# Unread products in TensorE's gaps, and batch-norm statistics eight tiles behind, in the last two graph layers

## The chip, the cores and the metric

The kernel runs on one core of a Trainium2 chip. The metric is the device time of one execution in microseconds (us); lower is better. Engines are named as in the profile: PE (TensorE), DVE (VectorE), ACT (ScalarE), POOL (GpSimd), SP (SyncE). PSUM is the memory that PE writes its products to[...]; SBUF holds everything else.

## The reference

A network of four layers on a graph of 3125 nodes with 256 features and 50,000 edges, all in f32. Each layer is a graph step and a feed-forward step. The change touches the graph steps of layers 2 and 3:

```python
def _L2_gnn_ref(h, w, snorm_n, edge_src, edge_dst, W_self, W_func, W_att):
    h_s = h @ W_self.T
    z = h @ W_func.T
    e = leaky_relu(concatenate([z[edge_src], z[edge_dst], w]) @ W_att.T)[:, 0]
    m = segment_max(e, edge_dst, num_segments=N)
    e_exp = exp(e - m[edge_dst])
    alpha = e_exp / segment_sum(e_exp, edge_dst)[edge_dst]
    agg = segment_sum(alpha[:, None] * z[edge_src], edge_dst)
    h_new = relu(where(deg > 0, h_s + agg, h))
    return h + h_new

def _L3_gnn_ref(x, edge_index, W_proj, b_proj, W_l, b_l, W_r, gamma, beta):
    xp = relu(x @ W_proj.T + b_proj)
    agg = segment_max(xp[src], dst)              # over the edges into a node, itself included
    out = relu(agg @ W_l.T + b_l + x @ W_r.T)
    # then a batch norm: mean and variance of each feature over all nodes, gamma, beta
```

Around them, `x = x + gnn(layernorm(x))`. Layer 2's feed-forward step is a mixture of 16 experts, two per node; layer 3's has 8.

## The kernel before, in words

**Tiles and rounds.** The nodes are sorted by in-degree and cut into 25 tiles of 128 (one node per partition). Edges are handled in *rounds*: round r of a tile takes the r-th in-edge of each of its 128 nodes. A tile has `RND[t]` rounds, from 32 for the first tile to 9 for the last, 413 in all; `OFF[t]` is a tile's first round. One round is one indirect DMA issued by POOL (`gather`, L138): 128 rows of a table in HBM land in one SBUF row buffer. Edges beyond a tile's rounds are handled apart.

**Order.** The order of instructions on each engine is the order in which the program records them. In layer 2 a small planner (`class Plan`) settles it while the kernel is built. Each chain of work is a generator that yields its next step as an engine, a planned duration and what it needs; the planner keeps a free time for each engine, takes the step that can start first (on a tie of 0.05 us the chain of lower rank), records it, and adds a delay to its end (0.35 us for PE). Buffers that several chains use are `Ring`s, whose slots hold the planned time at which they come free. The chains are:

- `gathers()`: the 413 gathers of layer 2 into blocks of 4 rows (`g_rows`), for all tiles in the order `order2`.
- `attend()`: for each tile transposes the normalised features (`tp`, copied by ACT to `a_xt`), multiplies them with `W_self` on PE (`pu`, L2250, in a PSUM bank of its own), forms the edge scores on DVE, their exponential on ACT (`g_e`, L2271), the sum of weights and the division on DVE, adds the self-product (L2278, DVE reading `pu` in PSUM) and then adds each gathered row times its weight (L2283).
- `route2()`: layer norm, gate logits and the sorting of nodes to experts, for groups of tiles; `moved` is the time at which all of it is planned.
- `ex2.tokens()`, `ex2.weights(...)` and `experts2()`: the experts' loads, products and combination, in three chunks of tiles.

`pl.run(moved, ...)` runs them all up to the end of the routing; what is left of the experts runs in a second call, beside the projection that writes layer 3's table `tab3`.

**Layer 3** is a loop written out by hand over the 25 tiles. 24 gathers (`ROWS`) are issued ahead; then, for each round, DVE takes the running maximum (L2408) and POOL issues the gather 24 rounds further on (`look`), which needs that row buffer back. Before a tile's rounds PE transposes its features (`turned`, L1660, copied by ACT in L1662 to `g_xt`), after them the maxima (`g_at`); eight products (L2418 and L2420) and two ACT instructions (`c_y`, L2421) give the tile's outputs `Y`, features on the partitions. DVE's `bn_stats` of a finished tile (`stats`, L2397, two instructions of some 0.29 us) stands after the seventh round of a later tile, three tiles later (`LATE`); the last three tiles' statistics follow the loop, and then come the batch norm and the feed-forward step. PSUM there has three banks of `tp` and four of `mm`.

Of the kernel before, what the change touches and what calls it, by code (L numbers as in the profile page):

```python
# [9 lines left out]
F32 = mybir.dt.float32  # L10
# [25 lines left out]
ROWS = 24  # L36
W_BUFS = 2
GT = 5
LATE = 3
SLACK = 3.0  # L40
MM_COL = 0.0019
KEEP = max(1, N // 2) - 1
# [55 lines left out]
def tile_gnn_ffn(ctx: ExitStack, tc: tile.TileContext, a: dict, out: bass.AP):  # L98
# [7 lines left out]
    @contextmanager  # L106
    def psums(**bufs):
        with tc.tile_pool(name="psum", bufs=1, space=PSUM) as p:
            before = dict(banks)
            banks["pool"], banks["bufs"] = p, bufs  # L110
            yield
            banks.update(before)

    def ps(tag, shape):
        return banks["pool"].tile(shape, F32, name=tag, tag=tag, bufs=banks["bufs"][tag])
# [1586 lines left out]
    class Plan:  # L1702
# [4 lines left out]

        def __init__(self):
            self.free = {"PE": 0.0, "DVE": 0.0, "ACT": 0.0, "POOL": 0.0, "SP": 0.0, None: 0.0}
            self.wire, self.on, self.chains, self.born = 0.0, None, [], 0  # L1710

        def add(self, rank, chain):
            c = [rank, self.born, chain, None]
# [13 lines left out]
        def run(self, until=None, rings=()):  # L1727

            while self.chains:
                best, end = [], until is not None and until.t is not None  # L1730
                if end and not any(at.t is None for r in rings for at in r.slots):
                    break
                for c in self.chains:
                    engines, us, needs = c[3]
                    if end and any(isinstance(n, Ring) for n in needs):
                        continue
                    needs = [n if isinstance(n, float) else n.t for n in needs]
                    if None in needs:
                        continue
                    for k, engine in enumerate(engines if isinstance(engines, tuple) else (engines,)):  # L1740
                        best.append((max([self.free[engine], *needs]), k, engine, c))
                if not best:
                    raise RuntimeError([str(c[2]) + str(c[3]) for c in self.chains])
                first = min(b[0] for b in best)
                start, _, engine, c = min((b for b in best if b[0] <= first + 0.05), key=lambda b: (b[3][0], b[3][1], b[0], b[1]))
                self.free[engine], self.on = start + c[3][1], engine
                self.resume(c, start + c[3][1] + self.DELAY[engine])

# [409 lines left out]
    tab3 = dram.tile([NP, D], F32, name="tab3")  # L2158

    with tc.tile_pool(name="g2", bufs=2) as gp, \  # L2160
            tc.tile_pool(name="w2", bufs=1) as wp, psums(tp=2, mm=2, y=1, u=2, pu=1):
        ws = load_w(wp, a["L2_gnn_W_self"], "w_s")
        rw2 = load_w(wp, a["L2_ffn_gate_w"], "w_g")
        gb2 = bcast(a["L2_ffn_gate_b"], 16, wp, "w_gb")
# [49 lines left out]
                                                   op0=OP.mult, op1=OP.add)  # L2214
        rounds_beyond(wp, body2)

        order2 = list(range(NT - 1, CH2[2][1] - 1, -1)) + list(range(CH2[2][1]))
        pl = plan[0] = Plan()
        R = {"tp": Ring(2), "mm": Ring(2), "y": Ring(1), "u": Ring(2), "pu": Ring(1)}
        blocks = Ring(GR_BUFS)  # L2220
        xin, rows = {t: At() for t in order2}, {t: [] for t in order2}
        here, done, moved = {t: At() for t in order2}, {t: At() for t in order2}, At()
# [16 lines left out]
        def attend():  # L2239

            for t in order2:
                n = RND[t]
                xn = XN[:, t, :]
                xt = gp.tile([P, 2, P], F32, name="a_xt")
                f = yield from turned_steps(R["tp"], xt, xn, xin[t], 0.36)
                own = yield "PE", 2 * D * MM_COL, (f, R["pu"])
                pfree = R["pu"].take()
                pu = ps("pu", [P, D])
                for k in range(2):
                    nc.tensor.matmul(pu, xt[:, k, :], ws[:, k, :], start=(k == 0), stop=(k == 1))  # L2250
                h = gp.tile([P, D], F32, name="g_u")
                hf = yield "ACT", 0.5, (xin[t],)
                nc.scalar.activation(h, xn, AF.Copy, scale=hasnt[:, t : t + 1])
                e = gp.tile([P, RND[0] + 1], F32, name="g_e")
                nm = gp.tile([P, 1], F32, name="g_nm")
                dn = gp.tile([P, 1], F32, name="g_dn")
                u = ACC[:, t, :]
                while here[t].t is None:
                    yield None, 0.0, (here[t],)
                f = yield "DVE", 0.07, (here[t],)  # L2260
                nc.vector.tensor_copy(e[:, n : n + 1], M[:, t : t + 1])
                for r0, m, g, free, landed in rows[t]:
                    f = yield "DVE", 0.14, (landed,)
                    stt(e[:, r0 : r0 + m], g[:, :m, D], q2[:, t : t + 1], ewF[:, OFF[t] + r0 : OFF[t] + r0 + m],
                        op0=OP.add, op1=OP.add)
                f = yield "DVE", 0.51, (f,)
                stt(e[:, :n], e[:, :n], 0.01, e[:, :n], op0=OP.mult, op1=OP.max)
                nc.vector.tensor_reduce(nm, e[:, : n + 1], axis=AX.X, op=OP.max)
                nc.vector.tensor_scalar_mul(nm, nm, -1.0)
                f = yield "ACT", 0.3, (f,)  # L2270
                nc.scalar.activation(e[:, : n + 1], e[:, : n + 1], AF.Exp, bias=nm)  # L2271
                f = yield "DVE", 0.71, (f,)
                nc.vector.tensor_reduce(dn, e[:, :n], axis=AX.X, op=OP.add)
                stt(dn, den[:, t : t + 1], e[:, n : n + 1], dn, op0=OP.mult, op1=OP.add)
                nc.vector.reciprocal(dn, dn)
                nc.vector.tensor_scalar(e[:, : n + 1], e[:, : n + 1], dn, None, op0=OP.mult)
                f = yield "DVE", 0.41, (f, own)
                stt(u, u, e[:, n : n + 1], pu, op0=OP.mult, op1=OP.add)  # L2278
                pfree.t = f
                for r0, m, g, free, landed in rows[t]:  # L2280
                    f = yield "DVE", 0.52 * m, (f,)
                    for r in range(m):
                        stt(u, g[:, r, :D], e[:, r0 + r : r0 + r + 1], u, op0=OP.mult, op1=OP.add)  # L2283
                    free.t = f
                f = yield "DVE", 1.31, (f, hf)
                stt(u, u, has[:, t : t + 1], h, op0=OP.mult, op1=OP.add)
                stt(u, u, 0.0, xn, op0=OP.max, op1=OP.add)
                nc.vector.tensor_add(X[:, t, :], X[:, t, :], u)
                done[t].t = f
# [51 lines left out]
        with tc.manual_schedule(engines={EN.PE, EN.DVE, EN.Activation, EN.Pool, EN.SP}):  # L2341
            pl.add(2, gathers())
            pl.add(0, attend())
            pl.add(1, route2())
            pl.add(0, ex2.tokens())
            pl.add(0, ex2.weights((blocks, lambda: gp.tile([P, GB, ZW], F32, name="g_rows", bufs=GR_BUFS)
                                   .rearrange("p r d -> p (r d)"), here[order2[-1]])))
            ex2.out = "ACT"
            last = pl.add(4, experts2())
            pl.run(moved, R.values())  # L2350
            ex2.out = "ACT", "DVE"
            ex2.rest(range(NT))
            pl.meet(6.0)
            last[0] = 0
            order3 = ((20, 25), (15, 20), (10, 15), (6, 10), (3, 6), (0, 3))
            pl.add(3, ex2.fetch([t for g in order3 for t in range(*g)]))
            befores = [At(0.0), At(0.0)]
            for i, q in enumerate(order3):
                befores.append(At())
                pl.add(3 + i, table3(range(*q), f"t{i % 2}_", befores[i], befores[i + 2]))  # L2360
            pl.run()


    with tc.tile_pool(name="w3", bufs=1) as wp:
# [6 lines left out]
            return t  # L2371

        ga, be, bl = halves("c_ga", "L3_gnn_gamma"), halves("c_be", "L3_gnn_beta"), halves("c_bl", "L3_gnn_b_l")
        with tc.tile_pool(name="g3", bufs=2) as gp, psums(tp=3, mm=4):
            wl = load_w(gp, a["L3_gnn_W_l"], "c_wl")
            wr = load_w(gp, a["L3_gnn_W_r"], "c_wr")

# [18 lines left out]
                for i in range(2):  # L2396
                    nc.vector.bn_stats(bs[:, i, t, :], Y[:, i, t * P : t * P + h])  # L2397

            rows = {}
            with tc.manual_schedule(engines={EN.PE, EN.DVE, EN.Activation, EN.Pool, EN.SP}):  # L2400
                for r in range(ROWS):
                    look(r)
                for t in range(NT):
# [1 line left out]
                    xt = gp.tile([P, 2, P], F32, name="g_xt")  # L2405
                    turned(xt, XN[:, t, :])
                    for r in range(OFF[t], OFF[t + 1]):
                        nc.vector.tensor_tensor(u, u, rows.pop(r), op=OP.max)  # L2408
                        look(r + ROWS)
                        if t >= LATE and r == OFF[t] + 6:  # L2410
                            stats(t - LATE)
                    at = gp.tile([P, 2, P], F32, name="g_at")
                    turned(at, u)
                    for i in range(2):
# [4 lines left out]
                        for k in range(2):  # L2419
                            nc.tensor.matmul(py, wl[:, k, o], at[:, k, :], start=False, stop=(k == 1))  # L2420
                        nc.scalar.activation(Y[:, i, t * P : (t + 1) * P], py, AF.Relu, bias=bl[:, i : i + 1])  # L2421
                for t in range(NT - LATE, NT):
                    stats(t)


# [129 lines left out]
```

## Time and profile before

| | us |
|---|---|
| Median of 3 runs | 4231.69 (4225.03 to 4236.29) |
| The profiled execution, own time | 4194.93 |
| Its span, first to last instruction | 4193.1 |
| PE, DVE, POOL, ACT busy | 2681.7, 1935.3, 1758.2, 854.3 |
| Layer 2, gathers alone (2058 to 2380 us) | 322 |
| Layer 2, experts in three chunks and layer 3's table (2380 to 3149) | 769 |
| Layer 3, the gathering loop (3149 to 3747) | 598 |
| The rest of layer 3 (3747 to 4193) | 446 |

The profile is of one execution; stages are named by their place in its span. Busy is the time in which an engine worked. A group's line reads: kernel line, engine, operation, output<-inputs, shapes and count; then busy us in all, mean ns of one, and idle us just before them with what ended most of it. "remote" and "issue" are releasers that the profile can't place better: an event from elsewhere, or nothing that it shows. An f32 product of 128x256 appears as two rows. The mean granted TensorE clock over the span is 0.777 of full speed.

### The profile page before, as it was taken

The numbers are of one execution on the slowest core, as the hardware profiler recorded it, in microseconds if no ns is written. First come the engines' busy times: TensorE is split into PE (matmuls) and PEld (weight loads), VectorE is DVE, ScalarE is ACT, GpSimd is POOL, SyncE is SP. The second block draws the span as 40 slices with busy tenths as digits, with TensorE's granted clock in tenths as the row PEclk, the third lists the DMA queues.
The fourth block names the chain that finished last, engine by engine and source line by source line (L and its number), as shares of the span: only waits on it lengthen the run. The fifth ranks groups of instructions, "written<-read, shape, count | busy, mean of one in ns | idle before, by whom it ended". The sixth has DMA issues, their size and how long they took to land.

```text
span 4193.1 us, 46658 instructions
## 1 busy us (share of the span) xinstructions
PE 2681.7 (64%) x12940; PEld 2120.1 (51%) x12940; DVE 1935.3 (46%) x7465; ACT 854.3 (20%) x1839; POOL 1758.2 (42%) x1996
## 2 busy tenths in 40 slices
PE   1698999999889999948411366366670111137875
PEld 1576787777777878737310254254540011135653
DVE  4446666665665555442344433334563233245300
ACT  1121223221222233211100022022320000013321
POOL 4333334342253333002466545544337756633323
PEclk9678999989899999978755577577775555557987
DMA  6766455452243444113233355355523323323543
GB/s 220 230 185 205 129 149 159 124 149 63 81 125 102 118 131 128 52 48 107 74 95 93 84 177 177 90 173 173 177 83 104 103 76 91 94 74 109 161 159 101
DMA packets 275970, 521.46 MB, mean 124 GB/s; under 512 B 53608, under 2 KB 176896, under 8 KB 275684
## 3 DMA queue, kind: packets, MB, share of 16 engines
q0 software_dynamic: 105344, 306.57, 25.2%
q1 hardware_dynamic: 159466, 201.07, 15.5%
q10 hardware_dynamic: 10874, 10.54, 0.8%
q8 instruction: 114, 1.87, 0.2%
q14 instruction: 172, 1.41, 0.1%
HBM read 431.19 MB, written 86.78 MB: 124 GB/s over the span
## 4 chain that ended last, share of the span: by engine, by line
another core or an unknown queue 14%; PE 14%; issue 9%; DVE 6%; POOL 3%; DMA 3%; ACT 2%; DVEq 0%; POOLq 0%; ACTq 0%
PE y L1996 5%; PE mm L1992 5%; DVE ACC L2283 2%; DMA xg<-XX,ro_pos 1%; POOL xg L142 1%; PE tp L2047 1%; POOL g_row L138 1%; POOL ro_g L138 1%; PE u L1839 1%; DMA tab<-ACC,idI 1%; PE u L1984 1%; PE mm L2418 0%; ACT ro_h L2073 0%; PE tp L1777 0%
## 5 line engine op out<-in xcount | busy, mean ns | idle before, releaser
L138 POOL DMA_INDIRECT g<-tab,m_si x521 | 498.9, 958 | 978.7 <-DVE mt L897 527.7
L138 POOL DMA_INDIRECT g_rows<-tab,srcI x413 | 402.2, 974 | 287.5 <-DVE ACC L2283 124.6
L138 POOL DMA_INDIRECT g_row<-tab,srcI x413 | 397.7, 963 | 189.3 <-issue 111.1
L887 PEld LDWEIGHTS c<-s,g 128*128 128x128 f32 x2084 | 347.9, 218 | 150.1 <-issue 59.6
L887 PE MATMUL c<-s,g 128*128 128x96 f32 x2084 | 358.2, 301 | 84.1 <-issue 25.5
L894 PE MATMUL pw<-w_d,f 65*128 65x256 f32 x1042 | 375.6, 446 | 13.8 <-DVE mt L897 12.1
L926 PE MATMUL f<-w_rel,aT 128*126 128x256 f32 x1600 | 372.6, 383 | 0.0
L891 ACT COPY aT<-c 128x384 f32<-128x384 f32 (+1 forms) x323 | 236.7, 737 | 596.3 <-PE c L887 395.2
L926 PEld LDWEIGHTS f<-w_rel,aT 128*126 128x126 f32 x1600 | 300.0, 189 | 49.9 <-issue 5.4
L1992 PE MATMUL mm<-ro_xt,ro_w 128*128 128x192 f32 (+3 forms) x928 | 248.7, 420 | 101.9 <-ACT ro_h L2073 61.6
L897 DVE TENSOR_TENSOR mt<-pw,g 128x256 f32<-128x256 f32 x521 | 218.1, 419 | 164.6 <-PE pw L894 85.4
L1996 PE MATMUL y<-ro_w,ro_h 128*96 128x256 f32 (+2 forms) x1040 | 264.9, 410 | 39.9 <-issue 31.5
L2418 PE MATMUL mm<-g_xt,c_wr 128*128 128x128 f32 x200 | 48.6, 387 | 370.0 <-issue 259.3
L1992 PEld LDWEIGHTS mm<-ro_xt,ro_w 128*128 128x128 f32 x928 | 181.4, 218 | 152.1 <-ACT ro_h L2073 66.9
L2408 DVE TENSOR_TENSOR ACC<-ACC,g_row 128x256 f32<-128x256 f32 x413 | 174.0, 424 | 175.4 <-DMA g_row<-tab,srcI 145.2
L1996 PEld LDWEIGHTS y<-ro_w,ro_h 128*96 128x96 f32 (+2 forms) x1040 | 191.5, 190 | 93.2 <-issue 38.3
L2418 PEld LDWEIGHTS mm<-g_xt,c_wr 128*128 128x128 f32 x200 | 40.3, 281 | 377.8 <-issue 262.4
L1044 PE MATMUL w<-w,b_h 128*126 128x256 f32 x800 | 220.6, 401 | 7.3 <-issue 3.7
L142 POOL DMA_INDIRECT xg<-XX,ro_pos x100 | 101.8, 1018 | 292.4 <-issue 135.0
L2283 DVE SCALAR_TENSOR_TENSOR ACC<-g_rows,g_e,ACC 128x256 f32<-128x256 f32 x413 | 200.9, 486 | 47.8 <-DVE ACC L2283 21.6
L1035 PE MATMUL w<-xt,w 128*128 128x252 f32 (+1 forms) x832 | 218.7, 388 | 6.2 <-ACT xt L957 3.2
L894 PEld LDWEIGHTS pw<-w_d,f 65*128 65x128 f32 x1042 | 180.8, 217 | 17.0 <-DVE mt L897 14.2
(578 smaller groups left out, 4558.4 us busy)
## 6 DMA issues: line engine op xcount, KB each, us to landing
ro_w<-in_L_ffn_blocks SPq DMA_DIRECT2D x58, 514.0 KB
ro_w<-in_L_ffn_blocks SPq DMA_DIRECT2D x58, 512.0 KB
f<-in_attr_t SPq DMA_DIRECT2D x521, 32.5 KB
xg<-zero SPq DMA_DIRECT2D x78, 200.0 KB
b_at<-in_edge_attr SPq DMA_DIRECT2D x100, 125.0 KB
tabr<-v SPq DMA_DIRECT2D x12, 758.0 KB
g<-tab,m_si POOLq DMA_INDIRECT x521
g_rows<-in_L_ffn_blocks SPq DMA_DIRECT2D x14, 514.0 KB
```

Of the source, the lines that this page charges most:

```text
L138: return nc.gpsimd.indirect_dma_start(out=dst, out_offset=None, in_=table, in_offset=bass.IndirectOffsetOnAxis(ap=idx, axis=0))
L887: nc.tensor.matmul(pc[:, h, o : o + GW], g[:, h * P : (h + 1) * P], sums[k][0], start=True, stop=True)
L891: nc.scalar.copy(aT[:, :, :, b : b + n * GN].rearrange("p k r n -> p k n r"), pc[:, :, : n * GW].rearrange("p k (n r) -> p k n r", r=16))
L894: nc.tensor.matmul(pw, feats.pop(k), wd, start=True, stop=True)
L897: nc.vector.tensor_tensor(mt[0], pw, rows.pop(k)[:, D:], op=OP.mult)
L926: nc.tensor.matmul(cur["f"][:TN], aT[:, h, r, :], wrel[:, h, r, :], start=(r == 0 and h == 0), stop=(r == 15 and h == 1))
L1035: nc.tensor.matmul(ph, w["01"][:, e, k, i * P : (i + 1) * P], xt[:, k, : n * TN], start=(k == 0), stop=(k == 1))
L1044: nc.tensor.matmul(py, last[:, k, i * TN : (i + 1) * TN], w["02"][:, e - 1, k, :], start=(k == 0), stop=(k == 1))
L1992: nc.tensor.matmul(ph, w[:, o : o + P], xt[:, k, :], start=(k == 0), stop=(k == 1))
L1996: nc.tensor.matmul(py, h[:, i, s], w[:, i * D : (i + 1) * D], start=(i == 0), stop=(i == self.fc - 1))
L2283: stt(u, g[:, r, :D], e[:, r0 + r : r0 + r + 1], u, op0=OP.mult, op1=OP.add)
L2408: nc.vector.tensor_tensor(u, u, rows.pop(r), op=OP.max)
```

## The change

Layer 2 and layer 3 get products that nothing reads ("fills"), and layer 3's statistics move.

- *Layer 2.* Ahead of each step that it records on PE, the planner issues unread products of the identity with `W_self`, 512 columns each, into a PSUM bank `idle`: as many as 60% (`FILL`) of the gap since PE's previous step holds, at 0.9 us each. It does so up to the end of `pl.run(moved, ...)` only. The bank comes from `pu`: the self-product now goes to a slot of the ring `u`, ACT copies it to SBUF (`a_pu`, one buffer), and DVE reads it there.
- *Layer 3.* Ahead of each round's maximum PE multiplies the identity with the gathered row, 256 columns, twice, into one PSUM bank `idle`.
- *Layer 3's statistics.* `LATE` is 8. From tile 20 on a second tile's statistics stand after a tile's eleventh round where it has one (tiles 20, 21 and 22), so that 20 tiles' are in the loop and five follow it.

In the built order there are 184 fills in layer 2 and 826 in layer 3.

```diff
--- before.py
+++ after.py
@@ -36,7 +36,8 @@
 ROWS = 24
 W_BUFS = 2
 GT = 5
-LATE = 3
+LATE = 8
+FILL = 0.6
 SLACK = 3.0
 MM_COL = 0.0019
 KEEP = max(1, N // 2) - 1
@@ -1707,7 +1708,7 @@
 
         def __init__(self):
             self.free = {"PE": 0.0, "DVE": 0.0, "ACT": 0.0, "POOL": 0.0, "SP": 0.0, None: 0.0}
-            self.wire, self.on, self.chains, self.born = 0.0, None, [], 0
+            self.wire, self.on, self.chains, self.born, self.rest = 0.0, None, [], 0, None
 
         def add(self, rank, chain):
             c = [rank, self.born, chain, None]
@@ -1743,6 +1744,9 @@
                     raise RuntimeError([str(c[2]) + str(c[3]) for c in self.chains])
                 first = min(b[0] for b in best)
                 start, _, engine, c = min((b for b in best if b[0] <= first + 0.05), key=lambda b: (b[3][0], b[3][1], b[0], b[1]))
+                if engine == "PE" and self.rest is not None:
+                    for _ in range(int((start - self.free["PE"]) * FILL / 0.9)):
+                        self.rest()
                 self.free[engine], self.on = start + c[3][1], engine
                 self.resume(c, start + c[3][1] + self.DELAY[engine])
 
@@ -2158,7 +2162,7 @@
     tab3 = dram.tile([NP, D], F32, name="tab3")
 
     with tc.tile_pool(name="g2", bufs=2) as gp, \
-            tc.tile_pool(name="w2", bufs=1) as wp, psums(tp=2, mm=2, y=1, u=2, pu=1):
+            tc.tile_pool(name="w2", bufs=1) as wp, psums(tp=2, mm=2, y=1, u=2, idle=1):
         ws = load_w(wp, a["L2_gnn_W_self"], "w_s")
         rw2 = load_w(wp, a["L2_ffn_gate_w"], "w_g")
         gb2 = bcast(a["L2_ffn_gate_b"], 16, wp, "w_gb")
@@ -2214,9 +2218,12 @@
                                                    op0=OP.mult, op1=OP.add)
         rounds_beyond(wp, body2)
 
+        def rest():
+            nc.tensor.matmul(ps("idle", [P, 512]), ident, ws.rearrange("p k n -> p (k n)"), start=True, stop=True)
+
         order2 = list(range(NT - 1, CH2[2][1] - 1, -1)) + list(range(CH2[2][1]))
         pl = plan[0] = Plan()
-        R = {"tp": Ring(2), "mm": Ring(2), "y": Ring(1), "u": Ring(2), "pu": Ring(1)}
+        R = {"tp": Ring(2), "mm": Ring(2), "y": Ring(1), "u": Ring(2)}
         blocks = Ring(GR_BUFS)
         xin, rows = {t: At() for t in order2}, {t: [] for t in order2}
         here, done, moved = {t: At() for t in order2}, {t: At() for t in order2}, At()
@@ -2243,11 +2250,14 @@
                 xn = XN[:, t, :]
                 xt = gp.tile([P, 2, P], F32, name="a_xt")
                 f = yield from turned_steps(R["tp"], xt, xn, xin[t], 0.36)
-                own = yield "PE", 2 * D * MM_COL, (f, R["pu"])
-                pfree = R["pu"].take()
-                pu = ps("pu", [P, D])
+                f = yield "PE", 2 * D * MM_COL, (f, R["u"])
+                free = R["u"].take()
+                pw = ps("u", [P, 2, D])[:, 0, :]
                 for k in range(2):
-                    nc.tensor.matmul(pu, xt[:, k, :], ws[:, k, :], start=(k == 0), stop=(k == 1))
+                    nc.tensor.matmul(pw, xt[:, k, :], ws[:, k, :], start=(k == 0), stop=(k == 1))
+                own = free.t = yield "ACT", 0.42, (f,)
+                pu = gp.tile([P, D], F32, name="a_pu", bufs=1)
+                nc.scalar.copy(pu, pw)
                 h = gp.tile([P, D], F32, name="g_u")
                 hf = yield "ACT", 0.5, (xin[t],)
                 nc.scalar.activation(h, xn, AF.Copy, scale=hasnt[:, t : t + 1])
@@ -2276,7 +2286,6 @@
                 nc.vector.tensor_scalar(e[:, : n + 1], e[:, : n + 1], dn, None, op0=OP.mult)
                 f = yield "DVE", 0.41, (f, own)
                 stt(u, u, e[:, n : n + 1], pu, op0=OP.mult, op1=OP.add)
-                pfree.t = f
                 for r0, m, g, free, landed in rows[t]:
                     f = yield "DVE", 0.52 * m, (f,)
                     for r in range(m):
@@ -2345,10 +2354,10 @@
             pl.add(0, ex2.tokens())
             pl.add(0, ex2.weights((blocks, lambda: gp.tile([P, GB, ZW], F32, name="g_rows", bufs=GR_BUFS)
                                    .rearrange("p r d -> p (r d)"), here[order2[-1]])))
-            ex2.out = "ACT"
+            ex2.out, pl.rest = "ACT", rest
             last = pl.add(4, experts2())
             pl.run(moved, R.values())
-            ex2.out = "ACT", "DVE"
+            ex2.out, pl.rest = ("ACT", "DVE"), None
             ex2.rest(range(NT))
             pl.meet(6.0)
             last[0] = 0
@@ -2371,7 +2380,7 @@
             return t
 
         ga, be, bl = halves("c_ga", "L3_gnn_gamma"), halves("c_be", "L3_gnn_beta"), halves("c_bl", "L3_gnn_b_l")
-        with tc.tile_pool(name="g3", bufs=2) as gp, psums(tp=3, mm=4):
+        with tc.tile_pool(name="g3", bufs=2) as gp, psums(tp=3, mm=4, idle=1):
             wl = load_w(gp, a["L3_gnn_W_l"], "c_wl")
             wr = load_w(gp, a["L3_gnn_W_r"], "c_wr")
 
@@ -2396,7 +2405,7 @@
                 for i in range(2):
                     nc.vector.bn_stats(bs[:, i, t, :], Y[:, i, t * P : t * P + h])
 
-            rows = {}
+            rows, taken = {}, 0
             with tc.manual_schedule(engines={EN.PE, EN.DVE, EN.Activation, EN.Pool, EN.SP}):
                 for r in range(ROWS):
                     look(r)
@@ -2405,10 +2414,18 @@
                     xt = gp.tile([P, 2, P], F32, name="g_xt")
                     turned(xt, XN[:, t, :])
                     for r in range(OFF[t], OFF[t + 1]):
-                        nc.vector.tensor_tensor(u, u, rows.pop(r), op=OP.max)
+                        g = rows.pop(r)
+                        for _ in range(2):
+                            nc.tensor.matmul(ps("idle", [P, D]), ident, g, start=True, stop=True)
+                        nc.vector.tensor_tensor(u, u, g, op=OP.max)
                         look(r + ROWS)
                         if t >= LATE and r == OFF[t] + 6:
-                            stats(t - LATE)
+                            stats(taken)
+                            taken += 1
+
+                        if t > NT - 6 and r == OFF[t] + 10:
+                            stats(taken)
+                            taken += 1
                     at = gp.tile([P, 2, P], F32, name="g_at")
                     turned(at, u)
                     for i in range(2):
@@ -2419,7 +2436,7 @@
                         for k in range(2):
                             nc.tensor.matmul(py, wl[:, k, o], at[:, k, :], start=False, stop=(k == 1))
                         nc.scalar.activation(Y[:, i, t * P : (t + 1) * P], py, AF.Relu, bias=bl[:, i : i + 1])
-                for t in range(NT - LATE, NT):
+                for t in range(taken, NT):
                     stats(t)
```

## The prediction

> **What bounds the kernel now.** I read the page's busy times and slices first, then the groups of layer 3, the busy time by stage, and in the stages that the change touches the waits and the timeline.
>
> ```profile
> PE   1698999999889999948411366366670111137875
> POOL 4333334342253333002466545544337756633323
> PEclk9678999989899999978755577577775555557987
> L138 POOL DMA_INDIRECT g_row<-tab,srcI x413 | 397.7, 963 | 189.3 <-issue 111.1
> L2418 PE MATMUL mm<-g_xt,c_wr 128*128 128x128 f32 x200 | 48.6, 387 | 370.0 <-issue 259.3
> ```
>
> One slice is 105 us. In slices 20 to 22 (layer 2, gathers alone) and 31 to 36 (layer 3) PE is nearly idle and its clock is at half speed, while POOL is busiest. By stage (start:end, length, PE busy and instructions, then PEld, DVE, ACT, POOL, clock, DMA share):
>
> ```profile
> 2058.00:2380.00 322.00, 65.57 (x180) 40.15 (x180) 148.39 (x501) 24.36 (x71) 205.60 (x227) 0.50 0.33 91
> 2600.00:2688.00 88.00, 21.36 (x59) 11.69 (x57) 28.26 (x115) 7.16 (x21) 46.93 (x61) 0.52 0.29 87
> 3149.00:3747.00 598.00, 99.69 (x498) 87.88 (x498) 184.32 (x463) 34.18 (x98) 397.73 (x413) 0.55 0.32 91
> ```
>
> Layer 3 takes 598 us for 413 gathers. No engine is full: POOL works 398 us and DVE 184. The waits inside it (engine, line, releaser: us, times, longest):
>
> ```profile
> ACT c_y L2421 <- remote: 300.0, 21, 22.0
> DVE ACC L2408 <- DMA g_row<-tab,srcI: 145.2, 164, 10.3
> DVE c_bs L2397 <- ACT c_y L2421: 125.3, 14, 26.9
> DVE c_bs L2397 <- issue: 119.9, 8, 22.4
> POOL g_row L138 <- DVE ACC L2408: 75.8, 60, 20.0
> ```
>
> POOL waits 75.8 us for row buffers, and DVE 245 us in the statistics for ACT's `c_y`. A plain reading says: delay the statistics, and POOL runs at its own pace. The timeline disagrees. Columns: start, duration, engine, work, idle before and its releaser.
>
> ```profile
> 3328.63 0.37 ACT L2421 ACTIVATE c_y<-mm,c_bl 128x128 f32<-128x128 f32 x1 [22.02 <-remote]
> 3334.29 0.37 ACT L1662 COPY g_xt<-tp 128x256 f32<-128x256 f32 x1 [5.29 <-remote]
> 3339.90 0.37 ACT L1662 COPY g_at<-tp 128x256 f32<-128x256 f32 x1 [5.24 <-remote]
> ```
>
> ACT waits 22 us for the 8 PE instructions behind one `c_y` and over 5 us for the 2 behind a transposed copy: **2.8 us per PE instruction**, though PE's own rows show each done in under 1 us and long before. While POOL issues gathers back to back (one each 1.25 us, 18 to 20 in 25 us) PE's completions reach the others late; in 25-us windows without gathers they arrive at once. When POOL pauses they come in a burst. Timing the unbroken stretches with the pause that follows gives 86 gathers in 120.8 us, 62 in 86.5, 54 in 76: 1.40 us each, and 413 × 1.40 = 578 of the 598 us. So I read layer 3 as bound by about 1.40 us per gather, and POOL's waits as that backlog draining.
>
> **What the Trainium skill says.** "TensorE: Matmul & The Clock Gate", Part 1, has TensorE at half clock until some 3.4 us of sustained activity and throttled again after an idle window as long. The trace agrees: 2432 to 2436 us is fully busy at 0.50, 2436 to 2440 at 0.99, and the clock is back at 0.50 after some 4 idle us. The same page, Part 2 ("Single matmul latency" and "Back-to-back issue gap"), says that an isolated product pays the array's drain, and one in a stream hides it. The trace agrees: a 256-column f32 product (two rows) lasts 0.62 us by itself warm (L894) and 1.22 cold, while such products follow each other every 0.43 and 0.86. The page's "A second HAM failure mode" tells of a clock that oscillates where PSUM banks are cycled and PE idles briefly between groups. No run here shows that yet.
>
> ```profile
> 1525.04 0.62 PE L894 MATMUL pw<-w_d,f 65*128 65x256 f32 x2
> 3134.92 1.22 PE L2327 MATMUL u<-w_bp,ones 1*128 1x256 f32 x2
> 3136.07 2.07 PE L2329 MATMUL u<-w_p,t_xt 128*128 128x256 f32 x4
> ```
>
> **The change, part by part.**
>
> *Layer 3's fills.* 413 rows × 2 = 826 products of 128x256 are added on PE. In the changed kernel's instruction order each carries a wait on PE's own completion count, for the fill just before it, because `idle` has one PSUM buffer. The first of a pair waits for the row's DMA too. So they cannot stream: each costs an isolated product and its signal. I take 0.70 us warm and 1.30 cold (0.62 and 1.22 above, plus 0.08 for the signal, a guess that no row shows). Two per row are 1.4 to 2.6 us, beside 1.40 us per gather, so PE becomes the bound. PE also has 20 instructions of real work per tile (4 transposing, 16 for the products), 0.22 us each warm and 0.43 cold from the streaming spacings. A row buffer is now free only after PE has read it too, so POOL, 24 rows ahead, is held to PE's pace; ACT's copies and `c_y` queue behind the fills as well. The fills are 0.86 of each 1.4 us when warm and 1.73 of 2.6 cold; stages of before with PE about 65% busy had clocks of 0.73 to 0.78 (2380:2600, 2688:2930, 2930:3149), so I choose two thirds of the fills warm: 0.90 us each. 413 × 1.80 = 743, and 25 tiles × 20 × 0.29 = 145: 888 us in place of 598, **+290**. All warm: 578 + 110 = 688, +90. All cold: 1074 + 215 = 1289, +691. Late completions would add to either end; POOL slowed to a gather every 2 us leaves time for them (in layer 1, at 14 gathers per 25 us, about half are prompt), so I add nothing in the middle.
>
> *Layer 3's statistics.* Moved from three to eight tiles behind: DVE no longer stands 245 us for `c_y`, but POOL's waits were mostly drain. 598 − 578 = 20 is all that the 1.40 us leave, and I take **−10**. Five tiles instead of three are left for the end: 4 more bn_stats at 0.29 us, **+1**. No DMA moves with them, and POOL's and SP's queues keep their instructions and order.
>
> *Layer 2's fills.* The built order has 184 of 512 columns: about 133 in the gather-only stage in runs of up to 12, some 33 around 2600:2688, few beside the experts. They wait for each other alike. Four rows last 1.03 us warm (L1996 x4 near 2581) and 2.07 cold, so I take 1.1 and 2.15, where the planner assumed 0.9 and filled 60% of its gaps. Hence each run takes 73 to 143% of the planned gap, and its end delays the self-product, the routing's products, ACT's queue and the row blocks that POOL reuses. Half warm, 133 × 1.6 = 213 us go into 322 − 66 = 256 idle us: it fits in total, not gap by gap, **+40** (cold 286 us, +30 at least, and +200 if completions come as late as in layer 3; warm 146 us, and the clock then helps the next expert chunk, −20). Around 2600:2688, 33 × 1.6 = 53 into 67 idle us: **+10**.
>
> *The self-product.* ACT gets 25 copies of about 0.37 us, 9 us on an engine that idles over 290 of 322 us, and PE loses its wait for L2278 (62.5 us, two times 33, in which it had little else to do). The copy stands in ACT's queue before the exponential of its tile and waits for a PE completion; I take 0, and the bounds of the fills include it. DVE reads SBUF in place of PSUM: 0.48 us as the like L2283, nothing.
>
> **The sum.** 4194.9 (the profiled execution; its span is 4193.1 and 1.8 lie around it) + 290 − 10 + 1 + 50 = 4526. The median of the runs, 4231.7, stands 36.8 above the profiled execution, so 4563.
>
> **The rivals.**
> *A, the fills' waits set the pace* (0.60): 4563. Its ends: 4195 + 90 − 9 − 20 + 37 = 4293, and 4195 + 691 − 9 + 100 + 37 = 5014.
> *B, the self-waits cost next to nothing* (0.22): a row then needs 0.86 us of PE warm, plus 0.35 for the tile's share, under the 1.40 of the gather. What is left is −10 from the statistics and 0 to +60 for cold starts and layer 2: 4222 to 4292, likeliest 4250. For it: PE is idle 83% of layer 3.
> *C, faster* (0.12): the 1.40 us are the statistics' doing after all, fills under 0.63 us fit two to a gather, and POOL runs at the 1.27 us of its undisturbed stretches: 413 × 1.27 = 525 and 10 for the end, −63; with −10 in layer 2 from the warmer clock 4195 − 73 + 37 = 4159. It decides once a fill with its wait is under 1.27/2 us and completions are prompt. For it: POOL's waits of 75.8 us for DVE; against it: the 2.8 us per PE instruction, seen also in layer 1 around 1530 with PE fully busy and warm.
> *D, completions stay late* (0.06): a gather blocks them for 1.40 us and two cold fills follow, 4.0 × 413 = 1652, +1054, with +150 in layer 2: about 5430.
> That the change adds no fills is excluded: they are in the built order.
>
> **How the numbers follow.** 0.3% (13 us) is about what a measurement of this kernel can tell from no change. A and D are slower; B is 0.05 within it and 0.17 above. So faster 0.12, same 0.05, slower 0.83. The range, 4235 to 5015, is A with most of B, and leaves out C, D and B's lowest part, 0.2 together.
>
> **What would show it.** For A: layer 3 of 700 to 1300 us with PE the engine that POOL waits for (`g_row` released by PE), PE's fills apart by 0.7 to 1.3 us and not 0.43, DVE's statistics without waits. For B: layer 3 near 590 us, fills 0.43 apart, POOL still near 1.40 per gather. For C: gathers 1.27 apart throughout and a clock near 1. If fills stand 0.43 us apart, my reading of the self-wait is wrong; if PE's completions reach ACT at once beside unbroken gathers, that of the 1.40 us is.

## The result and the profile after

The changed kernel takes 4383.7 us (median, 4379.8 to 4388.9); the kernel before 4228.4 in the same comparison. The ratio is 1.037, with an interval from 1.035 to 1.039: **slower by 155 us**. Forecast were 4563 us: the sign and the place were right, the loss was forecast at more than twice its size.

The page of the changed kernel, the slices first and then the groups of layer 3:

```profile
PE   1788999989989999667465566567779999987975
POOL 4333333432343332013654545543445666632332
PEclk9778999998899999878687677788759999996987
L2419 PE MATMUL idle<-g_row,ident 128*128 128x256 f32 x1652 | 608.4, 452 | 74.6 <-issue 13.7
L139 POOL DMA_INDIRECT g_row<-tab,srcI x413 | 420.3, 1018 | 281.0 <-PE idle L2419 207.9
```

In slices 30 to 34 (layer 3's loop) PE is at nine tenths of its time and its clock at nine tenths or more, and POOL now waits for PE's reading of the rows. By stage (start:end, length, then the busy times of PE, PEld, DVE, ACT and POOL, clock, DMA share, GB/s), first the changed kernel and then the kernel before:

```profile
2063.30:2951.90 888.60, 545.15 (x1764) 305.79 (x1765) 338.97 (x1107) 135.85 (x373) 467.17 (x512) 0.75 0.42 121
2951.90:3194.40 242.50, 177.74 (x772) 126.96 (x770) 152.06 (x590) 70.68 (x198) 92.98 (x126) 0.79 0.46 147
3194.40:3931.20 736.80, 667.25 (x2150) 318.00 (x2150) 189.05 (x467) 33.95 (x99) 420.30 (x413) 0.93 0.26 74
```

```profile
2060.50:2908.40 847.90, 360.96 (x1462) 270.83 (x1463) 339.79 (x1110) 132.38 (x359) 467.55 (x511) 0.64 0.44 129
2908.40:3149.60 241.20, 166.87 (x709) 122.80 (x707) 151.94 (x587) 66.89 (x187) 92.48 (x126) 0.74 0.43 141
3149.60:3748.00 598.40, 99.84 (x498) 87.88 (x498) 185.32 (x467) 34.55 (x99) 397.73 (x413) 0.55 0.32 91
```

The stages are layer 2's gathers, the rest of layer 2, and layer 3's loop from its first gather to its last `c_y`. So layer 2 lost 42 us and layer 3 138 us; 3 more lie before and 2 after. That is the 185 us between the two profiled executions (spans 4378.1 and 4193.1). It is 30 us more than the medians differ by, because the profiled execution of before was 37 us faster than its median. So 42 and 138 each come from one pair of executions, and these 30 us may sit in either. The waits in layer 3 (engine, line, releaser: us, times, longest):

```profile
PEld idle L2419 <- PE idle L2419: 348.2, 723, 0.9
POOL g_row L139 <- PE idle L2419: 207.9, 287, 3.5
DVE c_bs L2406 <- ACT c_y L2438: 37.0, 5, 16.2
ACT c_y L2438 <- PE mm L2437: 21.4, 31, 1.8
```

A fill's weight load waits for the fill before it, 723 times. `c_y` no longer waits 22 us for PE: its longest wait is 1.8. In the timeline of a warm stretch (start, duration, engine, work, idle before and its releaser) the fills are 0.76 us apart, and there is one gather for two fills:

```profile
3596.36 0.30 PEld L2419 LDWEIGHTS idle<-g_row,ident 128*128 128x128 f32 x2 [0.46 <-PE idle L2419]
3597.12 0.30 PEld L2419 LDWEIGHTS idle<-g_row,ident 128*128 128x128 f32 x2 [0.46 <-PE idle L2419]
3597.34 0.95 POOL L139 DMA_INDIRECT g_row<-tab,srcI  x1 [0.49 <-PE idle L2419]
3597.88 0.30 PEld L2419 LDWEIGHTS idle<-g_row,ident 128*128 128x128 f32 x2 [0.46 <-PE idle L2419]
```

Only the first tile is different. Three stretches of it and the rest (start:end, length, PE busy and instructions, clock, DMA share, GB/s):

```profile
3198.00:3210.00 12.00, 11.48 (x20) 0.50 0.35 100
3222.00:3234.00 12.00, 2.44 (x4) 0.50 0.37 104
3246.00:3288.00 42.00, 40.14 (x66) 0.50 0.17 50
3300.00:3930.00 630.00, 585.82 (x2005) 1.00 0.26 75
```

PE starts cold (at half clock), with a fill each 1.28 us. After some 20 us of gathers 1.25 us apart, completions come late and a fill takes 5.6 us (3225.38, 3230.98, 3236.60 in the timeline). A completion is the semaphore update by which an engine tells the others that an instruction is done. POOL runs out of row buffers and stops, completions are prompt again, and still the clock stays at half speed until the first tile's own products at 3297. From there on it is 1.00 for 630 us.

**Two conditions.** The experiments ran on four chips on which the kernel before takes some 3745 us and not 4228, so every number of theirs is set against the before that ran beside it. The run e9_before_again shows what differs.

### The profile page after: what moved, and what is told of

It reads as the page before. It is cut to its first block, busy times and chain, and to the rows that moved or that the text cites. A ratio compares the mean times of both kernels' runs of the same rounds, so it can differ in the third digit from the quotient of the medians.

```text
span 4378.1 us, 51091 instructions
## 1 busy us (share of the span) xinstructions
PE 3438.5 (79%) x14960; PEld 2381.3 (54%) x14960; DVE 1936.6 (44%) x7465; ACT 860.4 (20%) x1864; POOL 1780.9 (41%) x1996
## 3 DMA queue, kind: packets, MB, share of 16 engines
q8 instruction: 130, 2.13, 0.2%
## 5 line engine op out<-in xcount | busy, mean ns | idle before, releaser
L2419 PE MATMUL idle<-g_row,ident 128*128 128x256 f32 x1652 | 608.4, 452 | 74.6 <-issue 13.7
L139 POOL DMA_INDIRECT g_row<-tab,srcI x413 | 420.3, 1018 | 281.0 <-PE idle L2419 207.9
L2419 PEld LDWEIGHTS idle<-g_row,ident 128*128 128x128 f32 x1652 | 258.8, 197 | 416.8 <-PE idle L2419 348.2
L2222 PE MATMUL idle<-w_s,ident 128*128 128x512 f32 x368 | 249.6, 766 | 124.6 <-remote 94.5
```

Of the source, the lines that this page charges most:

```text
L139: return nc.gpsimd.indirect_dma_start(out=dst, out_offset=None, in_=table, in_offset=bass.IndirectOffsetOnAxis(ap=idx, axis=0))
L2222: nc.tensor.matmul(ps("idle", [P, 512]), ident, ws.rearrange("p k n -> p (k n)"), start=True, stop=True)
L2419: nc.tensor.matmul(ps("idle", [P, D]), ident, g, start=True, stop=True)
```

## The experiments

### The kernel before and the changed one, once more

No edit in either. 

> The kernel before, unchanged, profiled beside the experiments, because the runs that came with the experiments on single parts give it 3744 us and not 4228. Theory, POOL's gathers no longer make PE's completions late where it takes 3744 us: no wait of ACT for c_y of 20 us, gathers 1.25 us apart, layer 3's loop 515 to 530 us. Rival, something else is faster there (PE's clock, DMA): gathers still 1.40 us apart in layer 3 and the gain lies in other stages.

Measured: 3756.6 us, one run; 23 others of the same kernel beside it have a median of 3748.9. Layer 3's loop and layer 2's gathers by stage, and then one of layer 3's waits:

```profile
2834.90:3359.50 524.60, 107.84 (x498) 100.48 (x498) 187.19 (x471) 35.65 (x99) 391.88 (x413) 0.56 0.36 104
2002.50:2612.00 609.50, 334.13 (x1518) 259.13 (x1518) 353.45 (x1161) 133.96 (x368) 469.23 (x511) 0.70 0.60 183
```

```profile
ACT c_y L2421 <- PE mm L2420: 63.5, 50, 1.3
```

The longest wait of `c_y` for PE is 1.3 us where it was 22, with the clock as cold as before (0.56) and gathers 1.25 us apart from end to end. Of PE's instructions that report their completion, 99.9% have a semaphore record within 0.1 us of their end here; in the profile that the prediction read it is 70%, and for 15% of them that trace holds no record at all. The work itself is the same: DVE is busy for 1938.4 us here and 1935.3 there, POOL for 1753.1 and 1758.2, and the DMAs move 521.46 MB in both. So late completions are a condition of that chip or time, not of the program.

Nor are they PE's alone, as the prediction has it. Of DVE's instructions 73% have their record within 0.1 us there and 99.8% here, of ACT's 78% and 100%. In layer 3 DVE waited 18.1 us, in 22 waits, for its own preceding maximum (L2408); here it never does. Where completions are prompt the loop needs 1.27 us a row with its end counted in, and layer 2's gathers take 609.5 us in place of 847.9.

> The changed kernel, unchanged. Theory, PE's chain of fills takes the same time whatever the completions do: layer 3's loop 715 to 745 us, and layer 2 costs nothing where completions are prompt, so that the time is 185 to 205 us above the kernel before where that takes about 3744 us (and some 156 above where it takes 4228). Rival, the loss is a fixed 156 us or 3.7% in both.

Measured: 3947.3 us against 3748.9, ratio 1.053 (1.051 to 1.055), **198 us slower**. Layer 3's loop takes 718.3 us and layer 2's gathers 609.9, as in e9_before_again. PE's chain in layer 3 is nearly the same length in both conditions; what it is measured against is not.

### The parts alone

Layer 3's part, with layer 2 of before (the two `psums` and loop edits of the diff, `LATE = 8`): 

> Layer 3 of the changed kernel (fills and late statistics) on layer 2 of the kernel before. Theory, each fill waits for the one before it and PE sets the pace: layer 3's loop is 735 to 745 us as in the changed kernel (first tile some 105 us cold, then 1.51 us a row and 2.7 a tile), the time 110 to 140 us above before. Rival, layer 2's fills leave the clock or the queues in a state that layer 3 pays for: layer 3 is under 700 us here and the rest of the loss needs both parts.

Measured: 3938.8 us against 3744.2, ratio 1.052 (1.049 to 1.055), 195 us slower; the loop takes 719 us. So the loss of e10_after_again is layer 3's, within what these runs can tell (195 and 198 us). The 110 to 140 us of the expectation were counted against the slower loop of before.

The statistics alone:

```diff
-LATE = 3
+LATE = 8
...
-                            stats(t - LATE)
+                            stats(taken)
+                            taken += 1
...
```

> The statistics eight tiles later, and no fills anywhere. Theory, layer 3 is bound by about 1.40 us a gather and POOL's waits of before were the backlog draining: the loop stays at 580 to 595 us, time 5 to 15 us under before. Rival, the statistics held DVE and so POOL: the loop falls to 525 to 545 us, time 50 to 70 us under before.

Measured: 3744.7 against 3744.2, ratio 1.001 (0.9996 to 1.0023); the loop takes 523 us. With prompt completions there is no wait for the statistics to remove, and this run can't tell the two theories apart. What they are worth where completions are late was not measured.

Layer 2's part alone, and only its new way of the self-product (`FILL = 0.0`): 

> Layer 2 of the changed kernel (fills and the self-product by way of ACT and SBUF), layer 3 of the kernel before. Theory, the two parts add: layer 3 starts 40 to 50 us later and then takes 598 us, time 30 to 50 us above before. Rival, the warm clock that layer 2's fills leave behind is a gain, and the loss comes from the join with layer 3: time within 13 us of before.

> Only the self-product's new way (ring u, ACT's copy to SBUF, DVE reading SBUF), with no fill in layer 2 and layer 3 of the kernel before. Theory, the fills cost layer 2's 45 us: time within 13 us of before, layer 3 starting within 10 us of 3150. Rival, the copy does it, since it stands in ACT's queue before the exponential and waits for a PE completion that comes late: time 30 to 50 us above before.

Measured: 3745.3 (ratio 1.0007, 0.9993 to 1.002) and 3743.2 (1.0003, 0.9988 to 1.0019). Neither costs anything here; layer 2's gathers take 608 us in both. The copy is free here, as costed. The fills' expectation of 30 to 50 us failed: the warm clock and the fills together are worth nothing in layer 2. The rival's number came true but not its reason, a loss from the join of the parts: e1_l3_fills_late8 has the loss without layer 2's fills.

Once more, beside a kernel with twice as large a share of each gap filled (`FILL = 1.2`, 404 fills for 184): 

> Layer 2's change alone once more. Theory, only late completions make its fills cost something: within 13 us of before where before takes about 3744 us, 30 to 50 us above where it takes about 4230. Rival, its cost depends on something else of the chip: a loss of over 20 us beside a before of 3744.

> Layer 2's change alone with twice the share of each gap filled (404 fills of 512 columns for 184). Theory, the late completions were the cost, not PE's time: 404 x 1.18 = 477 us of fills (warm) fit beside 609 us of layer 2's gathers only in part, so some loss is due, but under 60 us with prompt completions. Rival, each fill's time lies on the path: 220 more fills cost over 150 us.

Measured: 3743.4 against 3743.3 (1.0005, 0.9991 to 1.0019), and 3846.2 (1.028, 1.026 to 1.030), 103 us slower. The second lies between the two expectations: 220 more fills of 1.18 us are 260 us of PE, and layer 2's gathers grew by 98 (608 to 706). In its waits:

```profile
PEld idle L2222 <- PE idle L2222: 285.9, 321, 1.6
ACT a_pu L2260 <- PE u L2257: 184.1, 22, 29.1
```

PE waits in the fills, and ACT's copy waits up to 29 us for the self-product behind them. So 184 fills just fit into layer 2's gaps while completions are prompt. In the compared execution they did not, and there 94.5 us of idle time before these fills are released by "remote", a row that the prompt runs do not have. That late completions made the 42 us is therefore likely. It is not shown: no run under that condition took the fills out, and the 42 come from one pair of executions.

### What makes layer 3's fills expensive

Two PSUM banks for the fills, so that each waits for the last but one:

```diff
-psums(tp=3, mm=4, idle=1)
+psums(tp=3, mm=3, idle=2)
```

> Layer 3's fills and late statistics alone, with two PSUM banks for the fills (three for mm), so that a fill waits for the last but one. Theory, the wait for the fill just before is what costs: fills stream 0.43 us apart, 0.86 us a row, under POOL's 1.25, and the loop falls from about 720 to 520 to 550 us. Rival, the products themselves or the row buffers held by PE are the cost: the loop stays above 650 us.

Measured: 3745.2 against 3748.9, ratio 0.9998 (0.9986 to 1.0009): **the loss is gone**, with all 826 fills in place. The stage and POOL's wait for PE:

```profile
2817.00:3341.60 524.60, 475.39 (x2150) 350.47 (x2150) 186.52 (x467) 34.32 (x99) 392.61 (x413) 0.99 0.36 104
```

```profile
POOL g_row L138 <- PE idle L2410: 87.2, 286, 0.3
```

POOL waits for PE at most 0.3 us, the length of the pause that it has between gathers anyway. The clock is at 0.99, and the loop is exactly as long as that of before at 0.56 (524.6): a warm PE buys nothing here, because POOL's gathers set the pace.

One fill a row (`for _ in range(1)`): 

> As the changed layer 3, but one fill per gathered row. Theory, 0.76 us a row (1.28 cold) is under or at POOL's 1.25: the loop takes 520 to 550 us, and the time is within 25 us of before. Rival, any wait of POOL for PE's reading of the row delays the gathers: the loop stays above 600 us.

Measured: 3748.0, ratio 0.9998 (0.9986 to 1.0009); loop 526 us. A fill needs 0.76 us warm and 1.28 cold, and POOL's pace is 1.25 us a row, so PE keeps up. The clock wanders between 0.50 and 1.00 in windows of 20 us, of which two (start:end, length, PE busy and instructions, clock, DMA share, GB/s):

```profile
2855.00:2875.00 20.00, 19.13 (x33) 0.50 0.37 106
3295.00:3315.00 20.00, 13.52 (x59) 1.00 0.36 106
```

Fills that read a constant and not the row:

```diff
-nc.tensor.matmul(ps("idle", [P, D]), ident, g, start=True, stop=True)
+nc.tensor.matmul(ps("idle", [P, D]), ident, wl[:, 0, :], start=True, stop=True)
```

> Changed layer 3 on layer 2 of before, but the fills multiply the identity with a constant weight tile, so that no row buffer and no row's DMA is tied to PE; they still wait for each other. Theory, PE's own chain is the loop's length: it stays at 690 to 725 us although POOL issues its gathers 1.25 us apart and ends early. Rival, PE's hold on the row buffers makes the loss: the loop falls to 520 to 550 us.

Measured: 3939.7, ratio 1.051 (1.048 to 1.053). The stage, and POOL's wait for row buffers:

```profile
2836.00:3551.40 715.40, 666.72 (x2150) 317.49 (x2148) 187.62 (x467) 34.32 (x99) 392.35 (x413) 0.94 0.27 76
```

```profile
POOL g_row L138 <- DVE ACC L2411: 31.2, 27, 20.2
```

POOL no longer waits for PE; 400 of its gathers run some 1.25 us apart, and its last is issued 175 us before the loop ends. The loop is as long as ever. So POOL's 207.9 us of waits for PE in the changed kernel are a follow-up, and PE's chain is the cause.

One fill of 512 columns in place of two of 256:

```diff
-                        for _ in range(2):
-                            nc.tensor.matmul(ps("idle", [P, D]), ident, g, start=True, stop=True)
+                        nc.tensor.matmul(ps("idle", [P, 2 * D]), ident, wl.rearrange("p k n -> p (k n)"), start=True, stop=True)
```

> Changed layer 3 on layer 2 of before, but one fill of 512 columns (identity with a constant weight tile, not tied to the row buffers) per gathered row in place of two of 256: as many columns, half the waits. Theory, a fill that waits for the one before costs its columns, 0.43 us per 256 warm, and 0.33 once: 1.18 us a row warm as layer 2's fills in the changed kernel (2.1 cold), so PE's chain is 413 x 1.18 + 25 x 2.7 = 555 us and up to 30 more for a cold first tile, loop 550 to 590 us. Rival, the columns are the cost and not the number of waits: 700 us or more.

Measured: 3769.3 against 3743.9, ratio 1.008 (1.005 to 1.010), 25 us slower; loop 551 us, fills 1.18 us apart. As many columns with half the waits cost 25 us in place of 195. The spacings give the wait's price: 256 columns at 0.757 us, 512 at 1.18, so 0.43 for each 256 and **0.33 us for each wait** (warm, if each 256 columns cost the same in both). In e5_two_banks, where fills need not wait, most of their rows, two a fill, start 0.22 us apart, which is the same 0.43 to 0.44. e13 also carries no row's DMA wait, but e7_fill_const did not either.

The statistics at their old place, beside the fills (`LATE = 3`): 

> Layer 3's fills with the statistics three tiles later as before, layer 2 of before. Theory, the statistics' place is worth nothing beside the fills: within 0.3% of the same with eight tiles (3939 us where before takes 3744). Rival, with PE slower, c_y comes later and DVE stands in the statistics: 10 us or more slower than that.

Measured: 3935.2, ratio 1.052 (1.049 to 1.054); loop 719.5 us, as with eight tiles. Beside the fills their place is worth nothing either.

### The clock

A dense burst ahead of the first row:

```diff
+                for _ in range(20):
+                    nc.tensor.matmul(ps("mm", [P, D]), ident, wl[:, 0, :], start=True, stop=True)
```

> Changed layer 3 on layer 2 of before, with 20 unread 256-column products into the four mm banks ahead of the first row, which stream and so are dense. Theory, a chain of fills that wait for each other stays at the clock that it finds (in the changed kernel cold for 100 us, until the first tile's own products, then warm): fills 0.76 us apart from the first row on, first tile some 50 us in place of 87 to 105, loop 30 to 45 us shorter than without. Rival, the clock follows the share of time that PE works, whatever came before: the first tile stays at 1.28 us a fill, or the later ones fall back.

Measured: 3916.5, ratio 1.045 (1.043 to 1.047); the loop takes 692 us where e1_l3_fills_late8 takes 719. The stage, and the first tile in the timeline:

```profile
2831.00:3523.40 692.40, 643.71 (x2192) 312.81 (x2190) 188.55 (x467) 34.70 (x100) 417.62 (x413) 1.00 0.27 79
```

```profile
2841.80 48.27 PE L2412 MATMUL idle<-g_row,ident 128*128 128x256 f32 x128
```

The first tile's 64 fills (128 rows) take 48 us: 0.75 us each from the first on, against 1.28 without the burst. The chain stays at the clock that it finds. Shorter by 27 us and not by 30 to 45, since the burst itself takes 11 us.

## Why the prediction was wrong in size

The path was right. What failed is the size of its terms, above all the price of layer 3's chain: 888 us for a loop that measured 737.

**Right.** Each fill waits for the one before it, PE becomes the engine that POOL waits for, and the fills are 0.76 us apart warm and 1.28 cold where 0.70 and 1.30 were priced. The loop of 737 us and the fills' spacing are what the last section named for case A. e5_two_banks shows the cause by taking the wait away, and e7_fill_const excludes the row buffers. Of A's signs only "DVE's statistics without waits" failed: 37.0 us in 5 waits are left. The self-product's 0 held where completions are prompt.

**Near by luck, as far as the runs show.** Layer 2's +50 measured 42. It was priced as fills that overrun their gaps; where completions are prompt the same 184 fills cost nothing (e3_l2_change, e14_l2_again), so that price is not what made the 42.

**Wrong, in four terms.** The loss was forecast at 331 us (290 − 10 + 1 + 50) and is 155.

1. *"Two thirds of the fills warm"*, 743 us for 826 fills. In the trace 714 spacings are 0.757 us and 57 are 1.28. With 0.757 for the 55 fills next to a tile's own work or to a late completion, the fills are 655 us, 88 less. The step took the clock from stages whose PE was 65% busy in lumps. A chain at a steady 57% (0.43 of 0.76 us) keeps the clock that it has, and one dense burst is enough to set it; e12_warm_start shows that.
2. *The tile's work, "20 instructions ... 0.22 us each warm and 0.43 cold"*, 145 us. These instructions have 128 columns, and the price was that of a row of a 256-column product. From the last fill of a tile to the second of the next it is 3.8 us, 2.3 more (on average) than two fills' own spacing: 24 × 2.3 = 55 us, 90 less. The profile's own row (L2418, 128x128) named the width; the streaming spacing of 128 columns was not looked up.
3. *The statistics' −10* was not to be had once PE set the pace (e8_fills_late3: no difference). The late completions in the first tile (21 us) and the loop's two ends (6) are what is left: 888 − 88 − 90 + 27 = 737.
4. *"The median of the runs stands 36.8 above the profiled execution"* was carried over. For the changed kernel the median is 3.9 above its profiled execution (4379.8). That is 33 us of the 179 that separate forecast and measurement; 143 lie in layer 3, 5 in layer 2, 2 the other way at the end. Why the kernel before stood so far above its own profile is not known.

**The reading of the 1.40 us per gather** holds for that execution only. It was read as a property of the loop; e9_before_again has the same program at 1.25. The 75.8 us of POOL's waits for DVE's maxima (3.7 in e9_before_again), and DVE's 245 us in the statistics (2.2), were that condition's too. Rival C put 1.27 us a gather on prompt completions, and this came true without any edit, and then the statistics had nothing left to give (e2_late8). Case D's 4.0 us a row did not come about: once POOL is held back by PE, layer 3's completions are prompt, from 3240 on.

What made completions late in the compared executions is open. No experiment ran under that condition, so neither the statistics nor layer 2's fills were tried alone there.

## What to carry to other kernels

Before filler work goes onto an idle engine, ask what each piece waits for: with one buffer, even for output that nothing reads, the pieces wait for each other, and 0.33 us for each wait made a 0.86 us load 1.51 us and the idle engine the bound; a second buffer took all of it away. Ask too whether the engine that is to be made faster sets the pace: PE at full clock left the loop at 524.6 us. A stage that looks bound by waits should be profiled on a second chip before its waits are priced.

## What the runs showed of the hardware that was not expected

- The same program took 4228 us and some 3745 us with the same work on its engines. What sets the two apart in the profiles is when completions arrive beside back-to-back gathers: 70% of PE's and 73% of DVE's have their record within 0.1 us in one, 99.9% and 99.8% in the other. That this makes the whole difference is not shown.
- TensorE's clock has a memory: a chain of 256-column f32 products at 67% of the time (0.86 of 1.28 us, by the streaming spacings) stayed at half clock for 42 us, and the same chain at 57% (0.43 of 0.76 us) stayed at full clock for 630 us. A dense burst of 11 us moved it from the one to the other (e12_warm_start). With 512 columns a fill (e13_one_wide, 81% cold, 1.73 of 2.13 us) it was warm within some three fills: 385 of 412 spacings are the warm 1.18 us.
- The Trainium skill, "TensorE: Matmul & The Clock Gate", "A second HAM failure mode", tells of an oscillating clock in a bf16 kernel that cycles through PSUM banks, with PE idle briefly between groups of products. e6_one_fill shows such a clock with one bank and f32 (0.50 to 1.00 in 20-us windows, about half of the fills some 1.25 us apart); the chain of two a row does not, though it idles briefly between all its fills.
